# Background matmuls only after even slots, logarithms' matmuls first, and other slots for VectorE's own sums, in a tanh-attention kernel

## The chip, the cores and the metric

The kernel runs on one core of a Trainium2 chip. The metric is the device time in microseconds (us). The kernel before takes 6137.12 us, the median of three runs (6135.61, 6137.12, 6138.12).

## The reference, cut to what matters

Input x has 8 images of 128 channels by 36 x 36 pixels. Each image goes through a convolutional attention layer, and then, as 1296 tokens of 128 channels, through an attention whose scores are sums of tanh, and through a gated network of 64 experts. Nearly all of the time goes to the scores:

```
q = einsum('bld,ed->ble', x, Wq) + bq
k = einsum('bld,ed->ble', x, Wk) + bk
t = tanh(q[:, :, None, :] + k[:, None, :, :])
scores = einsum('bijd,d->bij', t, w) + bw[0]
attn = softmax(scores, axis=-1)
return einsum('bij,bjd->bid', attn, x)
```

For each image that is a tanh for 1296 x 1296 x 128 elements.

## The kernel before, in words

**Tanh by matmuls.** The kernel makes no tanh for the scores. The 128 channels are split in 16 groups of five and 8 groups of six. For a group with arguments z, the sum of w tanh(z) is n/d, where d is the sum of exp(s.z) over all sign patterns s of the group (32 for a five, 64 for a six) and n is the same sum with weights s.w. As exp(s.(q+k)) is a product of a part of q and a part of k, n and d are matmuls over 32 or 64 rows: the key features `kf` are the weights, and the query features `qf` (part 0 for d, part 1 for n) move through. TensorE (PE) can work on tiles of 32 or 64 rows side by side.

**Units and slots.** A *unit* is one image, one chunk of 432 queries (3 in an image) and one tile of 128 keys (10 in an image; an eleventh, of 16 keys, is worked on in a shorter unit of two slots). An ordinary unit has 12 *slots*, k = 0 to 11, two groups in each. In every three slots the first two are fives and the third is sixes, so k = 2, 5, 8 and 11 are sixes, and the "second fives" are k = 1, 4, 7 and 10. The kernel has 264 units, 240 of them ordinary, and 2928 slots; p numbers the slots through all units.

**What a slot does**, in the order in which the loop at the end of the program (L1113 on) issues it:

- `take_turns` (L1072): what background work has to do on other engines (evictions, above all).
- `numerators(p)`: the two n matmuls, each to a PSUM bank of a ring of four (`ps_n`). A matmul in float32 is two instructions on PE.
- `denominators(p + 3)` (L960): the d matmuls of the slot three ahead (LAG), to one of two double banks (`ps_d`); ScalarE (ACT) takes their logarithm (L972, out `lq`). After an odd slot's logarithm, ACT does one Exp with scale -1 (L975) over the pair of slots, so that `lq` then holds 1/d for both.
- `terms(p, ns)` (L982): VectorE (DVE) multiplies n by 1/d. In most slots the product goes to SBUF (`rp`, L1003) and GpSimd (POOL) adds it up (`accp`, L1010 and L1012). In four slots of a unit, `DVE_PAIRS`, DVE multiplies in place and also adds (`accd`, L992 to L999), which is four DVE instructions instead of two, and keeps the PSUM banks until the adds have read them.
- `matmul_turn` (L1077): background matmuls, if any are due.

At the end of a unit `sums` (L1016) lets POOL join the two sums, and seven slots later ACT takes their Exp.

**Background work.** Everything else (the next image's convolutions and its attention, key and query features, the weighing with the softmax, gates) is written as generators in four lanes: `first_of_all` (query features, and the scores of the short units), `urgent` (weighing), `gates`, `background`. A generator yields when its next piece is matmuls (`matmuls(rest)`) or something else (`step`, `TAKE`), each due `rest` slots later. Its PSUM tiles come from the same ring of four banks as n (`aux`). A *turn* is one such piece of matmuls. `matmul_turn` allows one turn after a slot; a lane other than `first_of_all` is held back while `balance` is negative, and in a slot before one of `DVE_PAIRS`. Each slot adds PACE = 400 columns to `balance` (never above 2 x PACE), and a turn takes off its columns (each matmul counts its columns, at least 128, plus 20). A turn's eviction, `TAKE = (False, 1)`, comes in `take_turns` of the next slot, or later where that is one of `DVE_PAIRS`.

**Engine order.** Each engine works through its instructions in the order of the program. So an n that waits for a bank holds back the d behind it on PE, and a logarithm that waits for its d holds back everything behind it on ACT.

The functions that the diff touches, and what calls them:

Of the kernel before, what the change touches and what calls it, by code (L numbers as in the profile page):

```python
# [45 lines left out]
NF = 8  # L46
FIVES = 4 * 5 * (NF // 2)

SLOTS = []
# [6 lines left out]
IN_TURN = [m + i for m in range(NF // 2) for i in (0, NF // 2)]  # L56
LAG = 3
SHIFT = 6.5
DVE_PAIRS = (2, 5, 8, 11)
PACE = 400  # L60

# [7 lines left out]
def kernel(  # L71
# [58 lines left out]
    with ExitStack() as loop, ExitStack() as score:  # L130
# [138 lines left out]

        TAKE = (False, 1)

        def step(rest=1):
            return (False, rest)
# [1 line left out]
        def matmuls(rest=0):  # L277
            return (True, rest)

        behind = [0]  # L280
# [656 lines left out]
        def new_block(b, c, q):  # L937
            qf = qfp.tile([128, 2, CH], F32, tag="qf", name="qf")
            qf_of[b, c, q] = qf
            return query_block(b, c, q, qf)  # L940
# [19 lines left out]
        def denominators(p):  # L960

            if p >= len(slots):
                return
            u, k = slots[p]
            d = ps_d.tile([128, 2, 512], F32, tag="d", name="d")
            n = banks(u, k)
            products(u, k, 0, [d[:, h, :] for h in range(n)])
            if k % 2 == 0:
                lq_of[u, k // 2] = lp.tile([128, 4, CH], F32, tag="lq", name="lq")
            lq = lq_of[u, k // 2]  # L970
            o = 2 * (k % 2)
            nc.scalar.activation(lq[:, o : o + n, :], d[:, :n, :CH], AF.Ln)  # L972
            if k % 2 == 1:
                some = lq[:, : o + n, :]
                nc.scalar.activation(some, some, AF.Exp, scale=-1.0)  # L975

        def numerators(p):
            ns = [ps_n.tile([128, 512], F32, tag="n", name="n") for _ in range(banks(*slots[p]))]
            products(*slots[p], 1, ns)
            return [ps[:, :CH] for ps in ns]  # L980

        def terms(p, ns):  # L982

            u, k = slots[p]
            lq = lq_of[u, k // 2]
            o = 2 * (k % 2)
            mult = nc.vector.tensor_mul
            rem = units[u][2] == NKT - 1
            if k in DVE_PAIRS and not rem:
                if k == DVE_PAIRS[0]:  # L990
                    live["d"] = acc.tile([128, CH], F32, tag="accd", name="accd")
                    mult(live["d"], ns[0], lq[:, o, :])  # L992
                    mult(ns[1], ns[1], lq[:, o + 1, :])
                    nc.vector.tensor_add(live["d"], ns[1], live["d"])
                else:
                    for h in range(2):
                        mult(ns[h], ns[h], lq[:, o + h, :])  # L997
                    for h in range(2):
                        nc.vector.tensor_add(live["d"], ns[h], live["d"])  # L999
            else:  # L1000
                rp = rpp.tile([128, 2, CH], F32, tag="rp", name="rp")
                for h, n in enumerate(ns):
                    mult(rp[:, h, :], n, lq[:, o + h, :])  # L1003
                if rem:
                    live.setdefault("rem", []).extend(rp[:, h, :] for h in range(len(ns)))
                elif k == 0:
                    live["r"] = rp
                elif k == 1:
                    live["p"] = acc.tile([128, 2, CH], F32, tag="accp", name="accp")
                    nc.gpsimd.tensor_add(live["p"], live["r"], rp)  # L1010
                else:
                    nc.gpsimd.tensor_add(live["p"], live["p"], rp)  # L1012
            if k % 2 == 1:
                lq_of.pop((u, k // 2))
# [23 lines left out]

        def rem_scores(p, u, rps):

            yield matmuls(1)
            ps = aux("rem")
            for h, rp in enumerate(rps):
                for i in range(TPC):
                    mm(ps[32 * i : 32 * i + 32, :T], by_key.rearrange("p x m -> p (x m)"),
                       rp[:, i * T : (i + 1) * T], start=(h == 0), stop=(h == len(rps) - 1))
            behind[0] += 3 * (T + 20)
            yield TAKE
            exps(p + 2, u, ps[:, :T])
            yield matmuls()  # L1050
# [17 lines left out]
        balance = [0]  # L1068
# [3 lines left out]
        def take_turns(p, k):  # L1072
            for lane in lanes:
                if lane.due(p, False) and (k not in DVE_PAIRS or lane is first_of_all):
                    lane.run(p)

        def matmul_turn(p, k):  # L1077


            before = behind[0]  # L1080
            for lane in lanes:
                while lane.due(p, True) and behind[0] == before:
                    paced = balance[0] < 0 or k + 1 in DVE_PAIRS
                    if lane is not first_of_all and paced or lane is gates and urgent:
                        break
                    lane.run(p)
            balance[0] = min(balance[0] - (behind[0] - before) + PACE, 2 * PACE)

        drain(normal(0))
        for name in ("wv_t", "wq_t"):  # L1090
# [9 lines left out]
        a_q, a_k, cs_s, fb_s, eb_s = (feat[n] for n in ("a_q", "a_k", "cs_s", "fb_s", "eb_s"))  # L1100
        drain(tokens(0), keys(0, order[:1]))
        for i, q in enumerate(IN_TURN):
            if i < 3:
                drain(new_block(0, 0, q))
            else:
                first_of_all.append(new_block(0, 0, q))
# [6 lines left out]
        for p, (u, k) in enumerate(slots):  # L1113
            b, c, j = units[u]
            rem = j == NKT - 1
            if k == 0:
                prefetch(u + 2)
                if c == 0 and j == 1:
                    if b > 0:
                        gates.append(gating(b - 1))  # L1120
                    if b == NB - 1:
                        gates.append(residuals(4))
                    if b + 1 < NB:
                        background.extend(
                            (normal(b + 1), conv_keys(b + 1), layer0(b + 1), tokens(b + 1),
                             keys(b + 1, range(NKT)))
                        )
            take_turns(p, k)
            ns = numerators(p)
            denominators(p + LAG)  # L1130
            terms(p, ns)
            if pending and pending[0][0] <= p:
                exps(p, *pending.popleft()[1:])
            last = p + 1 == len(slots) or slots[p + 1][0] != u

            if j == order[-1] and u + 1 < len(units) and k % 3:
                used = IN_TURN.index(SLOTS[k][0]) + 1
                if used < NF:
                    first_of_all.append(new_block(*units[u + 1][:2], IN_TURN[used]))
            elif j == order[-2] and last and u + 2 < len(units):  # L1140
                first_of_all.append(new_block(*units[u + 2][:2], IN_TURN[0]))
            matmul_turn(p, k)
            if last and rem:
                first_of_all.append(rem_scores(p, u, live.pop("rem")))
            elif last:
                pending.append((p + 7, u, sums(u)))
# [211 lines left out]
```

The softmax here doesn't subtract the row's maximum and nothing guards it: scores larger than these inputs give would overflow.

## Time and profile before

| | |
|---|---|
| median of three runs | 6137.12 us |
| the profiled execution's span | 6139.0 us |
| first n matmul to last n matmul (slots 0 to 2927) | 161.9 to 5986.7 us |
| mean time of an ordinary unit (240 of them, 12 slots each) | 23.83 us |
| a unit with no background in the last image (the quickest) | 19.9 us |
| matmuls n and d, L949, 432 columns | 11520 + 11520 instructions, of 574 and 561 ns, overlapping |
| logarithm L972, 128x864 | 2928 of 878 ns |
| Exp L975, 128x1728 | 1464 of 1638 ns |
| product L1003, 128x432 (two in a slot) | 3912 of 600 ns |
| product and add L997, L999, 128x432 | 1440 of 608 and 1440 of 602 ns |
| POOL's add L1012, 128x864 | 1440 of 2025 ns |

The profiled execution lies 1.9 us above the median. Times in the trace count from the span's start. In a row of a group the numbers after the bar are the busy time of the engine in us, the mean of one instruction in ns, and after the second bar the idle time of the engine just ahead of the group's instructions, with what ended most of it: "<-PE d L949 512.1" says that 512.1 us of it ended when the d matmuls of line 949 were done. PE is the matmul's stream, PEld the load of its weights, which runs ahead; a matmul's end is modelled.

### The profile page before, as it was taken

To read this page: it belongs to the slowest core of one execution; us is meant where nothing else is said; L and a number is where in the kernel's file an instruction comes from. 1 tells how busy PE (TensorE), PEld (TensorE's weight loads), DVE (VectorE), ACT (ScalarE), POOL (GpSimd) and SP (SyncE) were. 2 spreads that over 40 slices of the span, in tenths; PEclk is the share of its full clock that TensorE was granted. 3 is DMA by queue.
4 is the path that set the end of the run, shared out by engine and by line. 5 is a ranking of instruction groups with operands and counts; after the bars stand their busy time and mean duration, and the time that the engine had idled before them with its cause. 6 is when DMAs were issued, how large, how long until landed. Compare 5 with 4: busy or idle time off the path is not lost.

```text
span 6139.0 us, 93072 instructions
## 1 busy us (share of the span) xinstructions
PE 5957.9 (97%) x33480; PEld 2862.1 (47%) x33480; DVE 4796.4 (78%) x9521; ACT 5279.9 (86%) x5371; POOL 4597.7 (75%) x2819
## 2 busy tenths in 40 slices
PE   7999999999999999999999999999999999999996
PEld 5454444544544445444455444454444544544443
DVE  4787878877788787877888777887778877788882
ACT  1888898888988888889998889888898888999990
POOL 4777777777787777778778786877777777787870
PEclk9999999999999999999999999999999999999997
DMA  1210011100110002100111001110011100110008
GB/s 44 70 37 22 25 62 38 34 25 28 68 43 20 26 27 71 39 24 23 44 55 39 22 24 59 44 39 22 20 65 40 34 25 28 58 50 29 28 20 297
DMA packets 151519, 270.87 MB, mean 44 GB/s; under 512 B 45648, under 2 KB 76752, under 8 KB 151056
## 3 DMA queue, kind: packets, MB, share of 16 engines
q1 hardware_dynamic: 151056, 264.92, 13.0%
q8 instruction: 264, 4.33, 0.3%
q14 instruction: 199, 1.63, 0.1%
HBM read 200.41 MB, written 64.19 MB: 43 GB/s over the span
## 4 chain that ended last, share of the span: by engine, by line
PE 77%; ACT 7%; DVE 6%; issue 6%; POOL 2%; DMA 1%; SPq 0%; DVEq 0%; POOLq 0%; ACTq 0%
PE n L949 37%; PE d L949 12%; PE pa L284 7%; PE pc L284 5%; ACT lq L972 5%; PE s L284 3%; PE pk L284 3%; PE pq L284 3%; DVE rp L1003 2%; DVE n L997 1%; DVE accd L999 1%; PE d L954 1%; ACT lq L975 1%; DMA w<-in_weight_dram 1%; PE n L954 1%
## 5 line engine op out<-in xcount | busy, mean ns | idle before, releaser
L1012 POOL TENSOR_TENSOR accp<-accp,rp 128x864 f32<-128x864 f32 x1440 | 2915.8, 2025 | 1041.0 <-DVE rp L1003 948.8
L949 PE MATMUL n<-qf,kf 32*128 32x432 f32 (+1 forms) x11520 | 3325.3, 574 | 46.5 <-ACT e L1032 13.3
L949 PE MATMUL d<-qf,kf 32*128 32x432 f32 (+1 forms) x11520 | 2991.6, 561 | 38.7 <-ACT lq L972 38.2
L972 ACT ACTIVATE lq<-d 128x864 f32<-128x864 f32 x2928 | 2524.2, 878 | 542.6 <-PE d L949 512.1
L1003 DVE TENSOR_TENSOR rp<-n,lq 128x432 f32<-128x432 f32 x3912 | 2173.3, 600 | 743.5 <-PE d L949 542.8
L975 ACT ACTIVATE lq<-lq 128x1728 f32<-128x1728 f32 (+1 forms) x1464 | 2398.2, 1638 | 46.3
L949 PEld LDWEIGHTS n<-qf,kf 32*128 32x128 f32 (+1 forms) x11520 | 1206.4, 184 | 1600.3 <-DVE rp L1003 581.5
L949 PEld LDWEIGHTS d<-qf,kf 32*128 32x128 f32 (+1 forms) x11520 | 1090.0, 185 | 422.1 <-issue 224.7
L997 DVE TENSOR_TENSOR n<-n,lq 128x432 f32<-128x432 f32 x1440 | 814.9, 608 | 142.1 <-PE n L949 88.5
L999 DVE TENSOR_TENSOR accd<-n,accd 128x432 f32<-128x432 f32 x1440 | 866.3, 602 | 24.6
L1010 POOL TENSOR_TENSOR accp<-rp 128x864 f32<-128x864 f32 x240 | 485.2, 2022 | 197.7 <-DVE rp L1003 195.6
L711 POOL TENSOR_SCALAR qf<-qf,cs_s 128x432 f32<-128x432 f32 x192 | 260.9, 1365 | 45.0 <-ACT qf L710 44.4
L284 PEld LDWEIGHTS pa<-xh,e 128*108 128x108 f32 x1920 | 222.5, 174 | 131.1 <-DVE rp L1003 56.0
L1021 POOL TENSOR_TENSOR accd<-accp,accd 128x432 f32<-128x432 f32 x240 | 265.2, 1105 | 18.8
L1019 POOL TENSOR_TENSOR accp<-accp 128x432 f32<-128x432 f32 x240 | 264.4, 1102 | 16.7
L284 PE MATMUL pa<-xh,e 128*108 128x129 f32 x1920 | 262.9, 283 | 8.7 <-ACT e L1032 5.2
L284 PE MATMUL s<-q,k 128*116 128x432 f32 x480 | 230.3, 568 | 1.7 <-DVE q L316 1.4
L284 PEld LDWEIGHTS pk<-xT,a_k 128*128 128x128 f32 x1408 | 171.2, 192 | 107.0 <-DVE n L997 33.7
L462 POOL TENSOR_TENSOR tot<-tot,e 116x432 f32<-116x432 f32 x192 | 212.0, 1104 | 6.0 <-ACT e L471 4.6
L471 ACT ACTIVATE e<-s 116x432 f32<-116x432 f32 x240 | 124.9, 520 | 98.3 <-PE s L284 97.9
L284 PE MATMUL pa<-e,vw 116*128 116x432 f32 x480 | 204.6, 549 | 0.0
L284 PE MATMUL pk<-xT,a_k 128*128 128x128 f32 (+1 forms) x1408 | 202.5, 287 | 0.1
(213 smaller groups left out, 3788.4 us busy)
## 6 DMA issues: line engine op xcount, KB each, us to landing
kf<-kd SPq DMA_DIRECT2D x239, 512.0 KB
kd<-ks SPq DMA_DIRECT2D x158, 256.0 KB
w<-in_weight_dram SPq DMA_DIRECT2D x32, 1024.0 KB
wk_t<-wk_t_d SPq DMA_DIRECT2D x7, 768.0 KB
wv_t<-wv_t_d SPq DMA_DIRECT2D x7, 768.0 KB
wq_t<-wq_t_d SPq DMA_DIRECT2D x7, 768.0 KB
x<-in_x_dram SPq DMA_DIRECT2D x8, 648.0 KB
t<-tokd SPq DMA_DIRECT2D x96, 54.0 KB
```

The lines of the kernel that those rows point to most:

```text
L284: mm(out, lhsT, rhs, **kw)
L711: nc.gpsimd.tensor_scalar(qf[:, 1, :], qf[:, 0, :], cs_s[:, q : q + 1], None, ALU.mult)
L949: mm(outs[h][:, :CH], kf[rows[h], q, :], qf_of[b, c, q][rows[h], part, :], start=True, stop=True)
L972: nc.scalar.activation(lq[:, o : o + n, :], d[:, :n, :CH], AF.Ln)
L975: nc.scalar.activation(some, some, AF.Exp, scale=-1.0)
L997: mult(ns[h], ns[h], lq[:, o + h, :])
L999: nc.vector.tensor_add(live["d"], ns[h], live["d"])
L1003: mult(rp[:, h, :], n, lq[:, o + h, :])
L1010: nc.gpsimd.tensor_add(live["p"], live["r"], rp)
L1012: nc.gpsimd.tensor_add(live["p"], live["p"], rp)
L1019: nc.gpsimd.tensor_add(s[:, 0, :], s[:, 0, :], s[:, 1, :])
L1021: nc.gpsimd.tensor_add(d, s[:, 0, :], d)
```

## The change

It has five parts, and the matmuls, products and sums themselves stay.

1. `matmul_turn` runs background turns only after slots with even k. There it goes on as long as a lane has a due turn and `balance` is not negative, so that several turns can follow one slot, and it runs a turn's eviction at once (`TAKE` with rest 0). Each slot adds PACE = 370, up to 3 x PACE. The rule on slots before `DVE_PAIRS` goes.
2. In each slot `denominators(p + LAG)` comes ahead of `numerators(p)`.
3. `DVE_PAIRS` becomes (1, 4, 7, 10), the second fives; it was (2, 5, 8, 11), the sixes. POOL's first add of a unit is at k = 2 instead of 1.
4. The next chunk's query features are queued by a table, `NEXT_AT`, at even slots; four of the first chunk's eight are made ahead of slot 0 instead of three.
5. `rem_scores` asks for its turn without a rest of one slot.

```
-DVE_PAIRS = (2, 5, 8, 11)
-PACE = 400
+DVE_PAIRS = (1, 4, 7, 10)
+NEXT_AT = {2: IN_TURN[1:2], 4: IN_TURN[2:3], 6: IN_TURN[3:4], 8: IN_TURN[4:5], 10: IN_TURN[5:7]}
+PACE = 370
...
-        TAKE = (False, 1)
+        TAKE = (False, 0)
...
-                elif k == 1:
+                elif k == 2:
                     live["p"] = acc.tile([128, 2, CH], F32, tag="accp", name="accp")
...
         def rem_scores(p, u, rps):
-            yield matmuls(1)
+            yield matmuls()
...
         def matmul_turn(p, k):
-            before = behind[0]
-            for lane in lanes:
-                while lane.due(p, True) and behind[0] == before:
-                    paced = balance[0] < 0 or k + 1 in DVE_PAIRS
+            balance[0] = min(balance[0] + PACE, 3 * PACE)
+            while k % 2 == 0:
+                for lane in lanes:
+                    paced = balance[0] < 0
                     if lane is not first_of_all and paced or lane is gates and urgent:
+                        continue
+                    if lane.due(p, True):
                         break
+                else:
+                    return
+                before = behind[0]
+                lane.run(p)
+                balance[0] -= behind[0] - before
+                while lane.due(p, False):
                     lane.run(p)
-            balance[0] = min(balance[0] - (behind[0] - before) + PACE, 2 * PACE)
...
-            if i < 3:
+            if i < 4:
                 drain(new_block(0, 0, q))
...
             take_turns(p, k)
+            denominators(p + LAG)
             ns = numerators(p)
-            denominators(p + LAG)
             terms(p, ns)
...
-            if j == order[-1] and u + 1 < len(units) and k % 3:
-                used = IN_TURN.index(SLOTS[k][0]) + 1
-                if used < NF:
-                    first_of_all.append(new_block(*units[u + 1][:2], IN_TURN[used]))
+            if j == order[-1] and u + 1 < len(units):
+                for q in NEXT_AT.get(k, ()):
+                    first_of_all.append(new_block(*units[u + 1][:2], q))
+            elif j == order[0] and k == 0 and u > 0:
+                first_of_all.append(new_block(b, c, IN_TURN[-1]))
```

## The prediction

> **What bounds the kernel now.** I read the page's busy shares first, then stretches of the trace, then what the waits of the busiest engine end on, then the timeline around such a wait.
>
> ```profile
> PE 5957.9 (97%) x33480; PEld 2862.1 (47%) x33480; DVE 4796.4 (78%) x9521; ACT 5279.9 (86%) x5371; POOL 4597.7 (75%) x2819
> ```
>
> PE's 97% is not a limit: a matmul counts as busy from its start to its modelled end, and these lie over each other (574 ns each, issued far closer). ACT is busy for 86% of the whole span, start and tail included. By stretches:
>
> ```profile
> core 0: us, PE busy (x) PEld busy (x) DVE busy (x) ACT busy (x) POOL busy (x), PEclk, DMA share, GB/s
> 3119.00:3856.00 737.00, 726.82 (x4087) 348.79 (x4085) 594.42 (x1180) 659.33 (x671) 570.64 (x346) 0.99 0.12 38
> 3166.00:3190.00 24.00, 22.38 (x115) 10.69 (x112) 22.06 (x47) 20.15 (x20) 19.21 (x12) 0.93 0.12 41
> ...
> 5830.00:5870.00 40.00, 39.02 (x201) 15.61 (x200) 34.74 (x66) 39.62 (x39) 32.83 (x19) 1.00 0.06 17
> ```
>
> The first row is one image (the fifth): ACT works for 659 of 737 us. The last row is a stretch without background work: there ACT works 39.6 of 40 us, so without background ACT alone is the limit. The change takes nothing from ACT and gives it nothing, so through the slots time is ACT's work plus ACT's idle time, and the question is what becomes of the 78 us of idle time in an image. The middle row is a unit in which DVE has more to do (22.1 of 24 us): there little can be won. What ends ACT's idle time:
>
> ```profile
> L972 ACT ACTIVATE lq<-d 128x864 f32<-128x864 f32 x2928 | 2524.2, 878 | 542.6 <-PE d L949 512.1
> L1003 DVE TENSOR_TENSOR rp<-n,lq 128x432 f32<-128x432 f32 x3912 | 2173.3, 600 | 743.5 <-PE d L949 542.8
> L975 ACT ACTIVATE lq<-lq 128x1728 f32<-128x1728 f32 (+1 forms) x1464 | 2398.2, 1638 | 46.3
> ```
>
> Nearly all of it stands ahead of the logarithm, which waits for its d. Which logarithms these are, the timeline of ACT tells:
>
> ```profile
> 3146.50 0.87 ACT L972 ACTIVATE lq<-d 128x864 f32<-128x864 f32 x1
> 3147.71 0.89 ACT L972 ACTIVATE lq<-d 128x864 f32<-128x864 f32 x1 [0.34 <-PE d L949]
> 3148.64 1.64 ACT L975 ACTIVATE lq<-lq 128x1728 f32<-128x1728 f32 x1
> 3150.24 0.89 ACT L972 ACTIVATE lq<-d 128x864 f32<-128x864 f32 x1
> 3152.36 0.89 ACT L972 ACTIVATE lq<-d 128x864 f32<-128x864 f32 x1 [1.23 <-PE d L949]
> 3153.29 1.64 ACT L975 ACTIVATE lq<-lq 128x1728 f32<-128x1728 f32 x1
> ```
>
> At 3147.61 PE begins a turn of 12 instructions (`pa`, 1.58 us) after slot k = 2; the logarithm whose d stands behind it is an even one, and ACT has an odd logarithm and the Exp to do meanwhile (2.5 us): it starts at 3150.24 with no idle time. The next turn, after k = 3, delays an odd logarithm. ACT has only an even logarithm (0.88 us) to cover it, and sits idle for 1.23 us.
>
> I put each logarithm of the 240 ordinary units beside what stands on PE between the n of the slot four before it and its own d. 1438 odd logarithms: 767 with a turn there have 421 us of idle time (0.549 each), 671 without have 96 us (0.142 each). 1437 even ones: 772 with a turn have 9 us, 665 without 4 us. So 530 of the 543 us are told apart, and **turns after odd slots account for 421 us**.
>
> **The change, part by part** (sum against the profiled span, 6139.0 us; the median is 1.9 us lower).
>
> *Turns only after even slots.* The 767 turns after odd slots go, and their logarithms become like the 671: 421 - 767 x 0.142 = 421 - 109 = 312 us gained. The same work now follows even slots. Its size, by the matmuls of an image in the trace, counted as the kernel counts, is 117,000 columns, over 183 even slots 640 each; PACE allows 2 x 370 = 740, so all of it gets done. A turn now has 623 on average, so about every even slot has a turn of the present size instead of 54% of them, and where turns are small (452 columns, 0.92 us on PE) two follow one another, 1.84 us. What hides them is the odd logarithm and the Exp, 2.5 us. Measured slack: an even logarithm with a turn ahead starts 0.86 us (median) after its d was done, so a turn 0.6 to 0.7 us longer is mostly covered. I count some 50 double turns an image from the sizes (72 pieces of 452 columns, 35 of 592, 20 of 296 or less) at 0.2 us, times 8: 80 us, and 10 us for longer bursts after a lull, 90 us lost. Ends: 0 (the 772 rows show 0.012 each) and 400 doubles x 0.92 = 368 us.
>
> *Evictions at once.* They stand on DVE and ACT behind the slot's own work, as before, and ahead of the next slot's. ACT's wait inside the 2.5 us. 0 taken; the other end is the slower rival.
>
> *Denominators first.* No instruction more or less. A d no longer stands behind the n of its slot, which waits for a bank:
>
> ```profile
> PEld n L949 <- DVE rp L1003: 581.5, 1032, 1.5
> ...
> PEld n L949 <- DVE accd L999: 198.5, 472, 1.6
> ...
> PEld d L949 <- ACT lq L972: 146.1, 199, 5.0
> ```
>
> It can take away what is left ahead of odd logarithms, 96 + 109 = 205 us, or nothing. Against that, n now stands behind the d that waits for its bank (146 us here, and 38 us on PE itself, 184 us), and DVE behind n. Whenever that d waits, ACT is behind and working, so this costs only where DVE is the limit: 0 taken, ends -205 and +184.
>
> The Trainium skill, "TensorE: Matmul & The Clock Gate", section "The mechanism", speaks against this part: matmuls run strictly in program order, so all that follows a waiting d is late by its wait. The trace agrees as far as it goes (after the n that waits, the d starts within 0.1 us, at 3016.70 after 3016.60 us). By the rule alone the sum would be 184 us worse.
>
> *Second fives for DVE's own sums.* Again 4 DVE instructions (2 x 608 + 2 x 602 ns) in four slots. They keep n's banks longer, and the next n but one waits. After a second five PE now has a slot of sixes (timeline: four n and four d instructions, 1.65 us), before it had a five (8 instructions, 0.9 us): 0.75 us more cover in four slots of a unit, for the 199 us above. It counts only where a held n delays a d; 0 taken, at most the 199 gained.
>
> *Query features, short units.* As many turns (192); one moves ahead of slot 0: 0.92 on PE and 0.61 on ACT. 2 us taken, ends 0 and 4 (1.37 us of POOL's multiply added).
>
> Sum: 6139.0 - 312 + 90 + 2 = 5919; less 1.9: **5917 us**, 3.6% faster. Idle time ahead of logarithms would fall from 543 to about 320 us.
>
> **Rivals.**
>
> *Larger gain.* d first also frees the odd logarithms (-205): 5917 - 205 = 5712. Units like that of the middle row hold back some of it; priced at 5760. For it: even logarithms show that ACT can run with 0.012 us of idle time each. Against: DVE at 92% in such units.
>
> *Smaller gain.* Double turns cost 0.92 us each after all (368 instead of 90, less what d first returns, about 150): 6050. For it: around 3271 us a burst of 24 short matmuls after an even slot cost ACT 0.84 us.
>
> *Nothing is won*: idle time only moves from odd to even logarithms: 0.549 x 767 again, 6137.
>
> *Slower: DVE's queue in even slots of its own sums.* At k = 4 and 10, 480 slots, DVE has 2.4 us of own sums, then evictions at once (0.3 to 0.7 us; before, turns were kept away from such slots and evictions were put off), then the next products, 1.1 us: 4.0 us and more, against 3.97 us for two slots now (23.83 / 6). The next n waits for a bank held to the last add: 1.0 us (its matmul) + 2.4 against a turn of 1.2 and a d of 0.9 on PE, so up to 1.3 us late, and the odd d behind it too. At 0.7 us each, 480 x 0.7 = 336 us: 5917 + 336 = 6253. It turns the change into a loss from 222 / 480 = 0.46 us a slot. Against it: d of the next slot now goes ahead of that n.
>
> **How the numbers follow.** Forecast 5917 (say 5850 to 5990): 0.42. Larger gain: 0.16. Smaller gain (5990 to 6125): 0.19. Nothing: 0.04. Slower: 0.19. The range leaves out half of the slower case and some of the larger gain: 5750 to 6210. 0.2% (12 us) is about what a measurement of this kernel can tell from no change. Faster 0.77, same 0.04, slower 0.19.
>
> **What would show it.** Right: L972's idle time near 320 us, most of it ahead of odd logarithms; ACT busy as before (5280 us); "PEld n <- DVE rp" lower; the image's stretch near 709 us. D first right: no d behind a waiting n of its own slot. Wrong: idle time ahead of even logarithms above 150 us (bursts), or "PEld n <- DVE accd" well over 199 us and DVE busy over 90% in an image (the slower rival). The prediction fails if ACT is held by something other than d, or if lulls pile up turns.

## The result and the profile after

The changed kernel takes 6149.35 us (median of 11 runs, 6146.59 to 6153.59) against 6135.61 us (11 runs, 6128.71 to 6140.72) for the kernel before: ratio 1.0024, interval 1.0015 to 1.0033. It is a quarter of a per cent **slower**, where 3.6% faster was forecast. Line numbers of the kernel after are one higher than before (d and n L950, logarithm L973, Exp L976, products L1004 and L998, own adds L1000).

The page of the kernel after, engines and then groups, in the columns of before:

```profile
PE 5798.3 (94%) x33480; PEld 2877.2 (47%) x33480; DVE 4793.5 (78%) x9521; ACT 5281.9 (86%) x5371; POOL 4600.4 (75%) x2819
...
L973 ACT ACTIVATE lq<-d 128x864 f32<-128x864 f32 x2928 | 2490.8, 881 | 548.2 <-PE n L950 343.3
L1004 DVE TENSOR_TENSOR rp<-n,lq 128x432 f32<-128x432 f32 x3912 | 2158.3, 599 | 655.8 <-PE n L950 559.5
L976 ACT ACTIVATE lq<-lq 128x1728 f32<-128x1728 f32 (+1 forms) x1464 | 2398.4, 1638 | 46.4
L950 PEld LDWEIGHTS d<-qf,kf 32*128 32x128 f32 (+1 forms) x11520 | 970.2, 185 | 1395.2 <-ACT lq L973 585.9
L950 PEld LDWEIGHTS n<-qf,kf 32*128 32x128 f32 (+1 forms) x11520 | 1262.1, 185 | 673.0 <-issue 293.5
```

ACT does the same work (5281.9 us, 5279.9 before) and waits as long ahead of its logarithms (548.2, 542.6 before). What changed is who waits for whom on PE. The last two rows of before were the other way round:

```profile
L949 PEld LDWEIGHTS n<-qf,kf 32*128 32x128 f32 (+1 forms) x11520 | 1206.4, 184 | 1600.3 <-DVE rp L1003 581.5
...
L949 PEld LDWEIGHTS d<-qf,kf 32*128 32x128 f32 (+1 forms) x11520 | 1090.0, 185 | 422.1 <-issue 224.7
```

Summed over every weight load of n that VectorE released, and every one of d that ACT released: n waited 1174 us for VectorE before and 251 after, d 177 us for ACT before and 855 after. The waits of the kernel after (total us, number, longest us) name both sides:

```profile
PEld d L950 <- ACT lq L973: 585.9, 746, 4.6
...
ACT lq L973 <- PE n L950: 343.3, 501, 2.7
PEld d L950 <- ACT lq L976: 200.5, 337, 1.4
...
PEld n L950 <- DVE rp L1004: 85.6, 261, 1.5
...
PEld n L950 <- DVE accd L1000: 64.9, 201, 0.9
```

I counted the idle time ahead of the logarithms of the 240 ordinary units as the prediction did, here with three of the experiments below:

```
us of idle time           before  after  turns alone  short bursts  d first + fives
even logarithms             13.5    222      189          188             71
odd logarithms             516.7    308      363          309            431
  of these k = 3 and 9       158    240       65          243            217
ACT busy, whole span        5280   5282     5309         5273           5268
```

The 421 us behind odd turns are gone, but the sum is 530 us on both sides: odd logarithms have 209 us less and even ones 209 us more. Two places hold most of it.

*Bursts after even slots.* Turns follow 1082 even slots with 804 columns each (before, 1551 slots of either kind with 564; all counted in the slots, as the kernel counts), since `balance` lets them pile up: 382 even slots have none. Behind bursts of more than 1250 columns, 150 even logarithms hold 88 us. Where the stretch from a turn's first matmul to the d behind it lasts 2 us or more (162 of them ahead of even logarithms, 16 before), the logarithms hold 124 us. One of them, PE and ACT:

```profile
3164.77 0.94 PE L289 MATMUL tp<-ident,t2T 128*108 128x128 f32 x4
...
3165.39 1.65 ACT L976 ACTIVATE lq<-lq 128x1728 f32<-128x1728 f32 x1
...
3166.82 0.94 PE L289 MATMUL tp<-ident,t 108*128 108x108 f32 x4 [1.11 <-DVE accd L1000]
...
3167.69 1.81 PE L950 MATMUL d<-qf,kf 64*128 64x432 f32 x4
...
3169.29 1.40 PE L950 MATMUL n<-qf,kf 64*128 64x432 f32 x4
...
3169.55 0.89 ACT L973 ACTIVATE lq<-d 128x864 f32<-128x864 f32 x1 [2.52 <-PE d L950]
```

Two turns follow slot 4; the second waits until VectorE's own adds give back a bank (1.11 us), the d of slot 8 stands behind it, and ACT idles for 2.52 us. Part of that is TensorE's granted clock (PEclk in these rows, the third column from the end), here and in the stretch shown next:

```profile
3168.00:3170.00 2.00, 2.00 (x6) 0.87 (x6) 1.71 (x5) 0.45 (x1) 1.82 (x1) 0.50 0.00 0
3611.00:3616.00 5.00, 5.00 (x29) 2.44 (x29) 4.04 (x9) 3.78 (x4) 4.92 (x4) 1.00 0.01 3
```

At a clock of 0.50 this d of sixes takes 1.60 us until the n behind it starts (3167.69 to 3169.29), against 0.83 us at 1.00 below. Ten of the 162 stretches touch such a time; they hold 22 of the 124 us.

*d, n of sixes, d.* At k = 3 and 9 the odd d stands behind the n of slot 11 or 5, which is sixes. In another stretch:

```profile
3612.42 0.99 PE L950 MATMUL d<-qf,kf 64*128 64x432 f32 x4
...
3613.25 0.89 PE L950 MATMUL n<-qf,kf 64*128 64x432 f32 x4
...
3614.07 0.63 PE L950 MATMUL d<-qf,kf 32*128 32x432 f32 x2
...
3615.11 0.89 ACT L973 ACTIVATE lq<-d 128x864 f32<-128x864 f32 x1 [0.76 <-PE n L950]
```

d(8), n(5) and d(9) follow each other: from d to d it is 1.65 us (0.84 to 0.94 at the other odd k, medians), and ACT, with 0.89 us of logarithm to do meanwhile, idles for 0.76 us. The row's "<-PE n" names the n that ends beside that d.

### The profile page after: what moved, and what is told of

Read it like the earlier page. It is cut to its first block, busy times and chain, and to the rows that moved or that the text cites. A ratio compares the mean times of both kernels' runs of the same rounds, so it can differ in the third digit from the quotient of the medians.

```text
span 6146.2 us, 92939 instructions
## 1 busy us (share of the span) xinstructions
PE 5798.3 (94%) x33480; PEld 2877.2 (47%) x33480; DVE 4793.5 (78%) x9521; ACT 5281.9 (86%) x5371; POOL 4600.4 (75%) x2819
## 4 chain that ended last, share of the span: by engine, by line
PE 66%; DVE 11%; ACT 10%; issue 7%; POOL 4%; DMA 1%; SPq 0%; DVEq 0%; POOLq 0%; ACTq 0%
PE d L950 25%; PE n L950 18%; ACT lq L973 7%; PE pa L285 6%; PE pc L285 5%; DVE rp L1004 4%; PE s L285 3%; PE pk L285 3%; DVE n L998 3%; POOL accp L1013 2%; PE pq L285 2%; DVE accd L1000 2%; DMA w<-in_weight_dram 1%; ACT e L1033 1%; PE n L955 1%
## 5 line engine op out<-in xcount | busy, mean ns | idle before, releaser
L950 PE MATMUL n<-qf,kf 32*128 32x432 f32 (+1 forms) x11520 | 3121.7, 560 | 16.2 <-DVE rp L1004 7.7
L950 PE MATMUL d<-qf,kf 32*128 32x432 f32 (+1 forms) x11520 | 2822.6, 568 | 161.5 <-ACT lq L973 161.2
L973 ACT ACTIVATE lq<-d 128x864 f32<-128x864 f32 x2928 | 2490.8, 881 | 548.2 <-PE n L950 343.3
L1004 DVE TENSOR_TENSOR rp<-n,lq 128x432 f32<-128x432 f32 x3912 | 2158.3, 599 | 655.8 <-PE n L950 559.5
L976 ACT ACTIVATE lq<-lq 128x1728 f32<-128x1728 f32 (+1 forms) x1464 | 2398.4, 1638 | 46.4
L950 PEld LDWEIGHTS d<-qf,kf 32*128 32x128 f32 (+1 forms) x11520 | 970.2, 185 | 1395.2 <-ACT lq L973 585.9
L950 PEld LDWEIGHTS n<-qf,kf 32*128 32x128 f32 (+1 forms) x11520 | 1262.1, 185 | 673.0 <-issue 293.5
L998 DVE TENSOR_TENSOR n<-n,lq 128x432 f32<-128x432 f32 x1440 | 811.6, 607 | 145.6 <-PE n L950 124.4
L1000 DVE TENSOR_TENSOR accd<-n,accd 128x432 f32<-128x432 f32 x1440 | 865.9, 601 | 24.6
L993 DVE TENSOR_TENSOR accd<-n,lq 128x432 f32<-128x432 f32 x240 | 144.9, 604 | 116.4 <-PE n L950 115.7
L285 PE MATMUL s<-q,k 128*116 128x432 f32 x480 | 213.5, 555 | 5.1 <-DVE accd L1000 3.1
```

The costliest lines, as they stand in the source:

```text
L285: mm(out, lhsT, rhs, **kw)
L950: mm(outs[h][:, :CH], kf[rows[h], q, :], qf_of[b, c, q][rows[h], part, :], start=True, stop=True)
```

## The experiments

Ratios are against the kernel before, timed beside each experiment. Two theories stood at first: that denominators first is a *bank* matter (n is kept from holding back d, so the order helps) and that it is an *order* matter (it is what puts n of sixes between two d).

**Parts of the change, taken away or alone.** e1, the kernel after with numerators first again:

```
-            denominators(p + LAG)
             ns = numerators(p)
+            denominators(p + LAG)
```

> The changed kernel with the numerators' matmuls ahead of the denominators' again; all else as changed. Order theory: in the changed kernel the n of the sixes of slots 5 and 11 stands on PE between the d of an even slot (k = 2, 8) and that of the next odd one (k = 3, 9), and the 240 us of ACT's idle time ahead of these two logarithms come from it. Here they fall below 60 us; but now the n of the sixes of slots 2 and 8 stands ahead of the d of k = 5 and 11, whose idle time rises from 32 us to 100 us or more; time 6060 to 6130 us. Burst theory: the idle time comes from several turns after one even slot (214 us ahead of even logarithms), whatever the order: 6140 to 6160 us. Bank theory: n waits for its bank ahead of d once more, so that idle time ahead of all odd logarithms rises: 6200 us or more.

6354.78 us, 1.0354 (1.0340 to 1.0368). The time is the bank theory's (6200 us or more). n's waits on VectorE's own adds rise from 64.9 us to

```profile
PEld n L950 <- DVE accd L1000: 372.2, 672, 1.8
```

The idle time at k = 3 and 9 falls from 240 to 66 us and that at k = 5 and 11 rises to 204, as the order theory has it, but k = 2 and 8 rise to 239, and its time (6060 to 6130 us) is far off.

e2, the kernel after with VectorE's own sums back in the sixes:

```
-DVE_PAIRS = (1, 4, 7, 10)
+DVE_PAIRS = (2, 5, 8, 11)
...
-                elif k == 2:
+                elif k == 1:
```

> The changed kernel with VectorE's own sums back in the sixes (2, 5, 8, 11); even turns and d first stay. Order theory: the idle time ahead of k = 3 and 9 stays near 240 us, and time within 1% of the changed kernel's (6090 to 6200 us). Bank theory (the second fives free the banks in time): n waits for VectorE's adds 100 us or more longer than in the changed kernel (65 us behind accd), and time rises to 6200 us or more. Burst theory: as the order theory.

6322.38 us, 1.0299 (1.0285 to 1.0313): the bank theory again, and more than the 1% that the order theory allows. n's waits on VectorE's adds rise from 64.9 to 228.2 us (151.7 at L1000, 76.5 at L995), and VectorE's own products now wait for their n: "DVE n <- PE n" is 608.9 us, 124.4 in the kernel after.

e3, both edits: turns, evictions and the table alone.

```
-DVE_PAIRS = (1, 4, 7, 10)
+DVE_PAIRS = (2, 5, 8, 11)
...
-                elif k == 2:
+                elif k == 1:
...
-            denominators(p + LAG)
             ns = numerators(p)
+            denominators(p + LAG)
```

> Only the turns after even slots (with the pace, the evictions at once and the table of query features); n first and VectorE's own sums in the sixes as before. The prediction's first term says that this alone brings 222 us (5917 us). Order theory: odd logarithms have little idle time but k = 5 and 11, where the n of a six stands ahead of d: idle time ahead of all logarithms 350 to 450 us, 5980 to 6080 us. Burst theory: 214 us ahead of even logarithms stay: 6050 to 6150 us. Bank theory: VectorE's adds in slots 2 and 8, which are followed by a turn, hold the banks of the next slot's n, which is ahead of d: 6200 us or more.

6219.56 us, 1.0135 (1.0121 to 1.0148): **the turns alone lose 83 us.** Odd logarithms keep 363 us, 330 of it on the 1384 without a turn ahead (0.238 each), even ones have 189. 237 us of the odd ones' stand at k = 5 and 11, where n of sixes is ahead of d, as the order theory has it; the time is the bank theory's.

e7, denominators first in the kernel before:

```
             take_turns(p, k)
+            denominators(p + LAG)
             ns = numerators(p)
-            denominators(p + LAG)
```

> The kernel before with the denominators' matmuls ahead of the numerators' as its only change. The prediction's term says 205 us gained to 184 us lost. Order theory: turns after odd slots still stand ahead of the d of odd slots, and with them the n of slots 5 and 11: idle time ahead of odd logarithms stays at 450 us or more, that ahead of k = 3 and 9 rises; 6140 to 6220 us. Bank theory: d no longer waits behind the n of its slot, idle time ahead of logarithms falls by 100 us or more; 5990 to 6080 us.

6288.69 us, 1.0243 (1.0229 to 1.0257), slower than either theory said. n's waits for VectorE fall from 1174 to 451 us, d's for ACT rise from 177 to 794:

```profile
PEld d L949 <- ACT lq L972: 459.7, 654, 4.9
...
DVE n L997 <- PE n L949: 428.8, 633, 6.5
PEld d L949 <- ACT lq L975: 182.3, 318, 1.2
```

The middle line is part of the price: VectorE's own products wait 428.8 us for their n (88.5 before). From here a third theory is in the expectations, the *traded wait*: the order takes n's wait for VectorE away and puts d's wait for ACT in its place, with n and the turns queued behind it.

e8, denominators first and own sums in the second fives, with the old turns (kept from the same slots as before):

```
-DVE_PAIRS = (2, 5, 8, 11)
+DVE_PAIRS = (1, 4, 7, 10)
+NO_TURN = (2, 5, 8, 11)
...
-                elif k == 1:
+                elif k == 2:
...
-                if lane.due(p, False) and (k not in DVE_PAIRS or lane is first_of_all):
+                if lane.due(p, False) and (k not in NO_TURN or lane is first_of_all):
...
-                    paced = balance[0] < 0 or k + 1 in DVE_PAIRS
+                    paced = balance[0] < 0 or k + 1 in NO_TURN
...
+            denominators(p + LAG)
             ns = numerators(p)
-            denominators(p + LAG)
```

> The kernel before with the denominators first and VectorE's own sums in the second fives; the turns' rules stay as they were (held back before the sixes). Order theory: as with the denominators first alone, 6140 to 6220 us. Bank theory: second fives are followed by sixes, whose d covers VectorE's adds, so that n's bank waits fall and time is 30 us or more below that of the denominators first alone.

6112.85 us, 0.9960 (0.9948 to 0.9973): 25 us faster than the kernel before, and 176 us faster than e7, as the bank theory has it (30 us or more).

e9, the second fives alone, that kernel with numerators first:

```
-            denominators(p + LAG)
             ns = numerators(p)
+            denominators(p + LAG)
```

> The kernel before with VectorE's own sums in the second fives as its only change; n first, turns held back before the sixes as before. With the runs so far this completes the square of d first (alone: 1.024 times before, with the second fives: 0.996). If the two parts only work together (with n first, a second five's adds hold the bank of the six's n, which stands ahead of the d of k = 4 or 5): 6200 us or more. If the second fives help by themselves: 6100 us or less.

6229.85 us, 1.0146 (1.0131 to 1.0161), the case in which the two parts only work together. Where the second fives help is in n's waits on VectorE's adds (L999 or L1000): 198.5 us before and 270.3 here, with n first; 247.3 in e7 and 37.0 in e8, with d first. Each of the three parts loses alone. Differences to the kernel before, and what denominators first does in each setting, by subtraction:

```
                       numerators first   denominators first   difference
old turns, sixes              0                +151               +151
new turns, sixes            +83                +185               +103
old turns, fives            +90                 -25               -115
new turns, fives           +218                 +14               -204
```

The new turns cost in every setting: +83, +34 (185 - 151), +128 and +38. Denominators first and the second fives pay only together.

**The places of the idle time.** e4, numerators first in slots 5 and 11 only:

```
+N_FIRST = (5, 11)
...
-            denominators(p + LAG)
-            ns = numerators(p)
+            if k in N_FIRST:
+                ns = numerators(p)
+                denominators(p + LAG)
+            else:
+                denominators(p + LAG)
+                ns = numerators(p)
```

> The changed kernel, but in the sixes of slots 5 and 11 alone the n goes ahead of the d. Order theory: the d of slots 3 and 9 now follow the d of slots 2 and 8 at once; idle time ahead of k = 3 and 9 falls from 240 to 60 us or less, that ahead of k = 2 and 8 rises (78 us now) by at most 80 us; time 6030 to 6090 us. Burst theory: even logarithms are late anyway: 6120 to 6160 us. Bank theory: the n of slots 5 and 11 waits for banks that VectorE's adds of slots 4 and 10 hold, now ahead of d: idle time ahead of k = 2 and 8 rises by 150 us or more, 6140 us or more.

6326.42 us, 1.0308 (1.0294 to 1.0322). k = 3 and 9 fall from 240 to 40 us, k = 2 and 8 rise from 78 to 440: there d now stands behind an n of sixes that waits for its banks (196.0 us on VectorE's adds, 64.9 in the kernel after). That is the bank theory's place and time (6140 us or more).

e5, both d ahead of the n of sixes:

```
-            denominators(p + LAG)
+            if k not in (0, 6) or p == 0 or slots[p - 1][1] not in (5, 11):
+                denominators(p + LAG)
+            if k in (5, 11):
+                denominators(p + LAG + 1)
```

> The changed kernel, but in slots 5 and 11 the d of the next slot too goes ahead of n: on PE d(8), d(9), n(5), n(6) instead of d(8), n(5), d(9), n(6). Order theory (240 us of idle time ahead of k = 3 and 9 are there because the n of a six stands between the two d): idle time ahead of k = 3 and 9 falls below 60 us and that ahead of k = 2 and 8 stays below 120 us, since no waiting n is ahead of them; time 5930 to 6030 us. Bank theory (the n of slots 5 and 11 is late because VectorE holds its bank, and all that follows is late with it): the idle time goes to k = 4 and 10 (45 us now, then 150 us or more); time 6080 to 6160 us.

6322.62 us, 1.0302 (1.0288 to 1.0316). k = 3 and 9 keep 31 us, but even logarithms have 507, and k = 4 and 10 rise from 46 to 304 us, the place that the bank theory named. Both edits that clear k = 3 and 9 pay more elsewhere; this time lies well above both expectations.

e6, no second held-back turn once 600 columns were run after the slot:

```
+            start = behind[0]
             while k % 2 == 0:
                 for lane in lanes:
-                    paced = balance[0] < 0
+                    paced = balance[0] < 0 or behind[0] - start > 600
```

> The changed kernel, but after a slot's first 600 columns no further held-back turn follows. Burst theory (of the 214 us ahead of even logarithms, the 159 bursts over 1250 columns have 88 us): idle time ahead of even logarithms falls from 222 to 120 to 150 us, time by as much, 6050 to 6080 us. Order and bank theories: the bursts cost little beside the sixes, idle time ahead of k = 3 and 9 stays near 240 us; time 6100 to 6150 us.

6113.16 us, 0.9961 (0.9949 to 0.9974), 36 us below the kernel after, with 34 us less ahead of even logarithms (222 to 188). The burst theory forecast 120 to 150 us there and 6050 to 6080 us: the bursts are real, and a small part.

e10, no turns after slots 4 and 10, whose own sums the slower rival feared:

```
-            balance[0] = min(balance[0] + PACE, 3 * PACE)
-            while k % 2 == 0:
+            balance[0] = min(balance[0] + PACE, 4 * PACE)
+            while k % 2 == 0 and k not in (4, 10):
```

> The changed kernel with turns only after slots 0, 2, 6 and 8 (credit up to 4 x PACE), none after 4 and 10, which VectorE's own sums fill and which stand two slots ahead of the d of k = 9 and 3. Order theory: without the turn the d of k = 8 and 2 are early, and so are those of 9 and 3, whose 240 us fall below 100 us. Burst theory: four turns of 960 columns on average instead of six raise the idle time ahead of even logarithms from 222 to 350 us or more. Together 6100 to 6180 us; below 6050 us if bursts cost little, above 6200 us if they are what counts.

6189.85 us, 1.0083 (1.0068 to 1.0098). The idle time at k = 3 and 9 goes (24 and 0 us), so a turn after slot 4 or 10 does take part in it; but even logarithms rise from 222 to 413 us, 302 of it on 373 behind more than 1250 columns. Both theories' places come true, and the time lies between. The turns have to go somewhere.

e15, e8 with one turn after any slot but 1, 5, 7 and 11, and no eviction put off:

```
-NO_TURN = (2, 5, 8, 11)
+NO_TURN = (1, 5, 7, 11)
...
-                if lane.due(p, False) and (k not in NO_TURN or lane is first_of_all):
+                if lane.due(p, False):
...
-                    paced = balance[0] < 0 or k + 1 in NO_TURN
+                    paced = balance[0] < 0 or k in NO_TURN
```

> Denominators first and second fives with the kernel before's one turn a slot, but turns kept away from slots 1, 5, 7 and 11 instead of 1, 4, 7 and 10, and evictions never put off. Order theory: the odd logarithms of k = 9 and 3, which follow the n of a six, no longer have a turn ahead of them too (139 and 78 us with the turn); even logarithms of k = 8 and 2 get one, which costs 0.07 us each: 6040 to 6100 us. Loop theory: a turn after slots 4 and 10, which VectorE's own sums fill, makes n and VectorE meet, 6110 us or more.

6138.83 us, 0.9997 (0.9988 to 1.0006), where the loop theory (the next paragraphs) put it. k = 9 falls from 139 to 57 us, k = 7 rises from 102 to 134, even logarithms from 71 to 122.

**Is ACT's idle time to be had at all?** The idle time had moved from place to place, and the time had not followed. The *loop* theory: PE and VectorE, tied to each other by the ring of banks, are a second limit just below the time, and take up what ACT gains. e11 takes most of the Exp from ACT in the kernel after, e12 the same in the kernel before.

```
-                some = lq[:, : o + n, :]
+                some = lq[:, : o + n, :16]
...
-            nc.scalar.activation(e[:, : d.shape[-1]], d, AF.Exp, bias=eb_s)
+            nc.scalar.activation(e[:, : d.shape[-1]], d, AF.Exp, bias=eb_s, scale=1e-12)
```

> The changed kernel with the Exp over a pair of slots cut from 1728 to 64 elements (so 1/d is left out for nearly all elements, and the scores' Exp is scaled to stay finite); ACT's work falls by about 2000 us. Traded-wait theory (d's wait for ACT took the place of n's wait for VectorE): d no longer waits, and time falls by 8% or more, below 5650 us, and by more than that of the kernel before with the same cut. Rival, PE and VectorE limit the changed kernel by themselves: 5850 us or more.

> The kernel before with the same cut of the Exp over a pair of slots (1/d left out for nearly all elements, the scores' Exp scaled). Traded-wait theory: its n still wait for VectorE's release of the banks ahead of d, so it gains less than the changed kernel, to 5650 to 5850 us. Rival, ACT's idle time has one cause in both: both fall to the same time within 1%.

5946.04 us, 0.9687 (0.9670 to 0.9703), and 5910.61 us, 0.9627 (0.9613 to 0.9642). The page of e11:

```profile
PE 5707.4 (96%) x33480; PEld 2914.9 (49%) x33480; DVE 4768.0 (80%) x9521; ACT 3475.6 (58%) x5371; POOL 4589.4 (77%) x2819
...
L973 ACT ACTIVATE lq<-d 128x864 f32<-128x864 f32 x2928 | 2566.8, 886 | 2016.4 <-PE n L950 1168.4
```

And that of e12:

```profile
PE 5735.1 (97%) x33480; PEld 2803.9 (47%) x33480; DVE 4776.5 (81%) x9521; ACT 3468.5 (59%) x5371; POOL 4587.3 (78%) x2819
...
L972 ACT ACTIVATE lq<-d 128x864 f32<-128x864 f32 x2928 | 2589.5, 886 | 2092.4 <-PE d L949 1989.8
```

In e11 ACT has 1806 us less to do (5281.9 - 3475.6), and 203 us of it come off the time (6149.35 - 5946.04); in e12 1811 us less, and 229 come off (6139.72 - 5910.61). Most of the rest turns into idle time ahead of the logarithms (2016.4 and 2092.4 us). The traded wait does not go away: in e11 d still waits 630 us for ACT (855 in the kernel after). The rivals in both expectations hold: **with a third of ACT's work gone the program still needs 5911 to 5946 us**, and the two kernels are within 1% of each other there.

e16, the same edit in e8:

> Denominators first and second fives under the old rules of turns (0.996 times before), with the Exp over a pair of slots cut to 64 elements (1/d left out for nearly all, the scores' Exp scaled). Loop theory: what these two parts gain, they gain in the loop of PE and VectorE, so that with ACT out of the way it is below the 5911 us of the kernel before with the same cut, by 25 us or more. Rival: they gain only by feeding ACT earlier, and end within 15 us of 5911 us or above it.

5974.37 us, 0.9731 (0.9718 to 0.9745), 64 us more than e12. The rival holds: with ACT out of the way e8's two parts cost 64 us, and yet they are 25 us faster as they are, so what they gain, they gain at ACT.

e13 leaves VectorE's seven adds a unit out of the kernel after, e14 out of the kernel before (1680 adds of 0.60 us, 1008 us):

```
-                    nc.vector.tensor_add(live["d"], ns[1], live["d"])
...
-                    for h in range(2):
-                        nc.vector.tensor_add(live["d"], ns[h], live["d"])
```

> The changed kernel with VectorE's adds of its own sums left out (L1000 and L995: 8 of 12 groups' sums lost in part, seven adds of 0.60 us less in a unit, about 1000 us of VectorE's work). Loop theory (n's banks, freed by VectorE, and PE's order set about 5900 us without ACT, and ACT adds 200): time falls by 2 to 5%, to 5850 to 6030 us, and the idle time ahead of logarithms with it. Rival, VectorE's hold on the banks is not what is waited for (in the changed kernel n waits only 65 us for accd): less than 60 us, 6090 us or more.

> The kernel before with VectorE's adds of its own sums left out in the same way. Loop theory: n waits 199 us for these adds here, ahead of its d, so it falls by as much as the changed kernel or more, to 5850 to 5990 us. Rival: less than 60 us, 6080 us or more.

5976.07 us, 0.9731 (0.9717 to 0.9744), and 6054.25 us, 0.9856 (0.9841 to 0.9871): 173 us off the kernel after, 86 us (6140.58 - 6054.25) off the one before. The loop theory's number for the kernel after holds; for the one before neither does. Without these adds the changed kernel is 78 us, 1.3%, the faster one. By these two runs its gain is there, and VectorE's sums take it up.

**Fewer own sums.** If so, less of VectorE's work should help. e17 lets it keep three slots and gives the fourth to POOL; e18 adds e6's limit.

```
-DVE_PAIRS = (1, 4, 7, 10)
+DVE_PAIRS = (1, 7, 10)
```

> The changed kernel with three slots of VectorE's own sums (1, 7, 10) instead of four: slot 4's two adds on VectorE (2 x 0.60 us) become one of POOL (2.0 us). Loop theory (VectorE's work takes up what the new order gives; leaving all seven adds out gave 173 us): 290 us less work for VectorE, a quarter to a third of that gain, 40 to 60 us: 6090 to 6110 us. Rival, POOL becomes the wait (five adds in a row in slots 2 to 6, 10 us, three buffers of rp): VectorE waits for POOL's accp 100 us or more, 6150 us or more.

> The same with the limit of 600 columns ahead of a further held-back turn. Loop and burst theories: the two gains add up, 36 and 40 to 60 us, 6055 to 6080 us, and it is the fastest of all complete kernels here. Rival, POOL becomes the wait: 6110 us or more.

6242.36 us, 1.0168 (1.0154 to 1.0182), and 6224.19 us, 1.0139 (1.0125 to 1.0153): slower. In e17 VectorE's product now waits for POOL's first add of a unit (6.4 us in the kernel after):

```profile
DVE rp L1004 <- POOL accp L1011: 182.2, 116, 4.6
```

That is more than the 93 us lost against the kernel after, though e17 saves VectorE 242 us of work. POOL, busy for 82% there (5086.9 us), had no room for it: the rival's case, if not the whole loss.

**The granted clock, a rival for the small differences.** None of these expectations looks at it. Within the slots the granted clock was 0.50 for 90 us of the kernel before, 109 of the kernel after, 102 of e8, 137 of e15, 87 of e12, 195 of e11, 133 of e16, 109 of e14, 72 of e13, 218 of e17 and 300 of e18 (1.00 the rest of the time). At half speed at most half of such a time can be lost (my estimate). So the clock can hold up to 10 of the 14 us between the two kernels, all of the 35 us between e11 and e12, 23 of e16's 64, 17 of the 26 between e8 and e15, 19 of the 78 between e13 and e14, 55 of e17's 93, and all of e18's 75 against the kernel after. No run holds the clock fixed. In e1 to e7 and e9 it stands at 0.50 for 85 to 171 us, at most 41 us lost more than in the kernel before, which changes no sign in the table.

## Why the prediction was wrong, point by point

**What bounds the kernel: the step that failed.** "Time is ACT's work plus ACT's idle time" is true of any engine, and it held (5281.9 + 864.3 = 6146.2). What failed is the reading that ACT alone is the limit, so that idle time taken away at one place comes off the time. The stretch behind it, 5830 to 5870 us, has no background work: there neither PE's turns nor VectorE's evictions press. In place of the 222 us to be gained, 209 us went from the odd logarithms and 209 came back ahead of the even ones, and in e4, e5, e10 and e15, which emptied single places, the idle time stood elsewhere and the time rose (e15 against e8, the others against the kernel after). e12 shows how little room there was: with 1,811 us less of ACT's work the kernel before still needs 5911 us, 229 us or 3.7% less. The forecast of 5917 us asked for nearly all of that (220) from an edit that leaves ACT's work whole; this alone doesn't rule the forecast out, but it makes it unlikely. The page doesn't show it: ACT at 86%, VectorE at 78% and POOL at 75%, in rings that wait for one another. The prediction's middle row, too, "a unit in which DVE has more to do", has a granted clock of 0.93, which I passed over.

**Turns only after even slots: -312 forecast; alone +83 measured.** That the 421 us behind odd turns would go was right. Two terms were wrong: in e3 odd logarithms have 153 us less, not 312, and even ones 175 us more, not 90. "Their logarithms become like the 671": the 671 odd logarithms without a turn were no fair sample. 185 of them are k = 5 and have 0.308 each, 58 are k = 1 and have 0.242, the other four k have 0.007 to 0.076, and in the last image, which has the least background, they have 0.074. With the turns moved, odd logarithms without a turn have 0.238 (e3) and 0.222 (after) instead of 0.142. And 90 us for double turns and lulls became 176 in e3 and 209 in the kernel after. "The odd logarithm and the Exp, 2.5 us, hide it" leaves out that a second turn waits for VectorE's bank (1.11 us in the example), and that 382 even slots without a turn leave their columns to others. "A turn now has 623" is too high: within the slots it is 564, so turns after "about every even slot" would have had to grow by 13%, and they grew to 804. In e3, L972's successor has 49 us more of idle time and ACT is busy 29 us longer; together the 78 us by which the span grew.

**Denominators first: 0 taken, ends -205 and +184.** Both signs came true: alone +151, with everything else changed -204. That -204 meets the end of -205 is luck: it was to come from odd logarithms, whose idle time is 26 us less than without this part (334 in e1, 308 after), while that of even ones is 118 less (340 and 222). "This costs only where DVE is the limit" was the wrong reason to take 0: n waits behind the waiting d, and VectorE's own sums, which start later by that, are late for the next n (428.8 us of waits of the products in e7, and n's waits on the adds rise from 198.5 to 247.3 us). The Trainium skill, "TensorE: Matmul & The Clock Gate", section "The mechanism", says that matmuls stay in program order. The prediction weighed such a wait at 184 us; alone, the part cost 151, so the queue was a better guide than my reason against it. With the second fives the sign turns, which only the runs showed.

**Second fives: 0 taken, at most 199 gained.** Alone +90; behind denominators first -176 (6112.85 - 6288.69). The reason given, cover by the sixes that follow, came true only with d ahead of n (n's waits on the adds: 37.0 us in e8, 270.3 in e9); the parts were priced one by one, and the sum of parts is not the change.

**Evictions at once, query features.** Not tried apart; they are in e3's 83 us.

**The rivals.** "Nothing is won", 0.04, came nearest: idle time moved from odd to even logarithms and to k = 3 and 9, 6137 us forecast. It names the movement and not what holds the idle time up; I gave it little because I saw no second limit. The smaller gain named the bursts, whose limit gives back 36 us (e6). The slower rival's place wasn't it: waits of n on own adds fell from 198.5 to 64.9 us, and turns kept away from slots 4 and 10 made it slower (e10).

**What was to show it.** "Idle time ahead of even logarithms above 150 us (bursts)" came (222). "PEld n <- DVE rp" fell as forecast (581.5 to 85.6), and was no sign of a gain: d's wait had taken its place.

**Open.** What sets the 5911 to 5946 us with ACT relieved isn't settled, so the loop theory is the likeliest reading and not shown: no engine but PE, whose ends are modelled, is above 81% there. PE's own work can be estimated from steps without waits: 0.94 us for d and n of fives, 1.65 us for sixes, and for the turns the median step of each kind of matmul, 1430 us in all. That makes about 4800 of the 5593 us of slots in e12, so PE alone does not fill them either. Why e4 and e5 lose as much as 170 us when they clear the place at k = 3 and 9 is shown only as far as where the idle time went.

## What to carry to other kernels

Before pricing an engine's idle time, cut that engine's work in an experiment and look at how far the time falls: here 1,811 us less of work gave 229, so an edit that only feeds this engine earlier had little to win. An order on one queue trades one wait for another; price it by what stands behind the new waiter, and try parts of such a change in pairs, since two that lose 151 and 90 us alone gained 25 together. The two complete versions that beat both kernels are e8 (0.9960) and e6 (0.9961). And read the granted clock beside every timeline: the example of a burst above owed some 0.8 us to it.

## What the runs showed of the hardware

The four matmuls of 32 rows of d(9) and n(6) start 0.02 us apart (first halves at 3614.07 and 3614.09 us, second halves at 3614.54 and 3614.55), though all of d stands ahead of all of n in the program as written. Between these two, d ahead of n is no gain in time: both take 0.94 us together (the turn behind them starts at 3615.01). The d of sixes takes 0.83 us by itself (3612.42 to 3613.25) and the n of sixes behind it 0.82 (to 3614.07): so it is the n of sixes that delays a d. At a granted clock of 0.50 such a d took 1.60 us (3167.69 to 3169.29).
